# A four-layer Mamba network on one core: six state buffers, the gated output in the gate's tile, second-layer weights before the scans, a first tile without GpSimd products, image edges cleared on VectorE

## The chip, the cores and the metric

The kernel runs on 1 core of one Trainium2 chip. The time of a run is device microseconds of that core; the time of a kernel is the median of several runs. Below, PE is TensorE, DVE is VectorE, ACT is ScalarE, POOL is GpSimd and SP is SyncE, which here only issues DMAs. "Clock" is the share of its full clock that TensorE was granted.

## What is computed

The reference runs four layers, one after the other, on an image batch of 4 x 96 channels x 64 x 64:

- Layers 0 and 2 ("mamba"): each image is a sequence of L = 4096 tokens of 96 channels. Two selective-scan blocks follow each other, then a fusion with pooled channels, a batch norm and a residual.
- Layer 1 ("SSD"): four scans in chunks, over rows and columns, forwards and backwards.
- Layer 3 ("ConvNeXt"): a 7x7 depthwise convolution, a layer norm and an MLP.

The change concerns the selective-scan block, cut here to its core (192 inner channels `d`, 16 states `s`), and the image buffers of layer 3:

```
xz = layernorm(seq) @ in_w;  xs, z = split(xz)
xc = silu(conv4(xs))
dt, Bm, Cm = split(xc @ xproj_w)
delta = softplus(dt @ dt_w + dt_b);  A = -exp(A_log)
dA  = exp(delta[..., None] * A)
dBx = delta[..., None] * Bm[:, :, None, :] * xc[..., None]
h[t] = dA[t] * h[t-1] + dBx[t]                     # for each d and s
y = einsum('blds,bls->bld', h, Cm) + Dp * xc
seq = seq + (y * silu(z)) @ out_w
```

## The kernel before, in words

`program` calls `mamba_fusion`, `ssd`, `mamba_fusion`, `convnext`. Everything is fp32. A framework turns data dependences into semaphores; where tiles of one pool share addresses with tiles of an earlier one, the later ones wait until the earlier are free. Each tile name has a number of buffers (`bufs`); a new tile takes the oldest buffer and waits for that buffer's last readers.

**A mamba layer.** `mamba_fusion` runs 32 steps: 4 images x 2 blocks x 4 pieces of 1024 tokens. A piece is held as two halves of 512 tokens side by side. The 192 x 16 recurrences of a step are 24 groups of 128 (8 channels x 16 states), in three thirds `j`, four quarters `q` and two halves `p`. `Scan.run` writes out by hand the order of one group after another on every engine, and ties it down: in iteration n it emits `load` (group n+5), `spread` (n+1), `decay` (n+2), `after` (n-1), `product` (n+2), `scan` (n), and pieces of the next step's front. For one group:

- `load`, SP: `da`, delta copied to all 16 states by two DMAs from DRAM.
- There are two kinds of group. In 17 of 24, PE spreads `du` = delta*x into the PSUM tile `bs` (`spread`, line 497) and DVE multiplies `bs` by B (line 520); ACT makes exp(A*delta) in `da` (line 110). In the other 7 (`dma` set: p = 1 with even q, and j = 2, q = 1) `du` also comes by two DMAs, POOL multiplies it by B (`product`, line 505), and ACT writes the exponential into `bs`.
- `scan`, DVE, line 525: one TENSOR_TENSOR_SCAN of 1024 elements into a state tile `hs`, of which there are 4 buffers.
- `after`, POOL, line 532: `hc` = `hs` * C; ACT copies the last column into `carry`.
- `sums`, PE, line 546: adds up the states of two groups at a time into the PSUM tile `py`. At the end of a third, `close` (DVE, line 563) multiplies `py` by the gate `z` into a tile `y` (2 buffers), which `project` (PE, line 576) multiplies by `out_w`.

**Before the scans.** `mamba_weights` is a generator that loads and prepares one block's weights: `w_ln`, `w_in`, `w_conv`; then the products on DVE for `w_conv` (line 671), zeroing (675, 681), small loads, `w_dd` (690), the 16 loads of `w_a`, `w_out`, and an exp. For the first block it runs at once; for the second block it is put into `later`, and one of its pieces is emitted in each iteration from group 24 on. `first_front` makes the first step's inputs: `rows` (line 391), the broadcasts `bc` of B and C (`spread`, line 399), the stores of delta and `du` to DRAM (`dd`, `dg`, line 405). `mamba_front` does it for the other steps, under the scans.

**Memory of a mamba layer.** One list in `Laid` gives the order in which tile names lie in SBUF: `h` and the first weights, `dbl`, `delta`, `rs`, `seldu`, `du`, `x`, `ua`, `bc`, `X`, `z`, `hs`, `da`, `y`, `hc`, and the rest.

**Layer 3.** `convnext` holds half-images with a border of 3 in four `band` tiles, each 96 x 2692. Lines 1724 and 1725 set all of each to zero on POOL; `load` then writes the 64 x 64 part (line 1741), for the first half-image on DVE.

Of the kernel before, what the change touches and what calls it, by code (L numbers as in the profile page):

```python
# [18 lines left out]
F32 = mybir.dt.float32  # L19
AF = mybir.ActivationFunctionType  # L20
ALU = mybir.AluOpType
# [4 lines left out]
B, C, HH, WW = 4, 96, 64, 64  # L26
L = HH * WW
P = 128
T = 512
# [16 lines left out]
NQU = QUART // HEIGHT  # L46
GS = 2
# [21 lines left out]
KS = 7  # L69
HALF = KS // 2  # L70
# [100 lines left out]
def mamba_front(tc, k, x_in, pools, wt, parts, c, h, made):  # L171
# [4 lines left out]
    nc = tc.nc  # L176
    work, psum, dram = pools
# [36 lines left out]
    x = made["x"] = work.tile([P, 3, T], F32, name="x", bufs=2)  # L214
    for j in range(3):
        pu = bank("pu")
        for tap in range(4):
            kk = C + 1 if tap == 3 else C
            for i in range(2):
                nc.tensor.matmul(  # L220
                    pu[HALFP * i : HALFP * (i + 1)],
                    lhsT=wt["conv"][:kk, tap, D0[j] : D0[j] + HALFP],
# [5 lines left out]
                    k.act.other(x, x, AF.Silu)  # L228
            yield

    z = made["z"] = work.tile([P, 3, T], F32, name="z", bufs=2)

    def gate(j):
        pz = bank("pz")
# [13 lines left out]
    for j in range(3):  # L248
        for i in range(2):
            half = ds(HALFP * i, HALFP)  # L250
# [71 lines left out]
def first_front(tc, k, x_in, pools, wt, parts, h, made):  # L322

    nc = tc.nc
    work, psum, dram = pools
    nc.vector.memset(h[:C, 0:3], 0.0)

    def bank(tag, bufs):  # L330
        return psum.tile([P, T], F32, tag=tag, name=f"f_{tag}", bufs=bufs)

    xs, into = ([a[:C, ds(of + n * T, T)] for n in range(2)] for a, of in ((x_in, 0), (h, 3)))
    for n, tag in enumerate(("po", "py")):
        pc = bank("mm", 2)[:C]
        nc.tensor.matmul(pc, lhsT=k.center, rhs=xs[n], start=True, stop=True)
        sq = work.tile([P, T], F32, tag="ua", name="sq", bufs=3)[:C]
        nc.scalar.activation(sq, pc, AF.Square)
        pv = bank(tag, 1)[:C]
        nc.tensor.matmul(pv, lhsT=k.mean, rhs=sq, start=True, stop=True)  # L340
        rs = work.tile([P, T], F32, name="rs", bufs=2)[:C]
        rsqrt(k.act, rs, pv, k.eps[:C])
        nc.vector.tensor_tensor(into[n], pc, rs, ALU.mult)
        nc.vector.tensor_scalar(
            into[n], into[n], wt["ln"][:, 0:1], wt["ln"][:, 1:2], ALU.mult, ALU.add
        )

    x, z = (work.tile([P, 3, T], F32, name=m, bufs=2) for m in "xz")
    made["x"], made["z"] = x, z

    def gate(j):
        pz = bank("mm", 2)
        for i in range(2):
            nc.tensor.matmul(
                pz[HALFP * i : HALFP * (i + 1)],
                lhsT=wt["in"][:, DIN + D0[j] : DIN + D0[j] + HALFP],
                rhs=h[:C, ds(3 + i * T, T)], start=True, stop=True,
            )
        k.act.other(z[:, j], pz, AF.Silu, back=False)

    def rows_of(pd, j):
        for i in range(2):
            half = ds(HALFP * i, HALFP)
            nc.tensor.matmul(
                pd[half], lhsT=wt["xproj"][half, j], rhs=x[half, j], start=(j == 0), stop=(j == 2),
            )

    pd = None
    for j in range(3):
        pu = bank("mm", 2)  # L370
        for tap in range(4):
            kk = C + 1 if tap == 3 else C
            for i in range(2):
                nc.tensor.matmul(
                    pu[HALFP * i : HALFP * (i + 1)],
                    lhsT=wt["conv"][:kk, tap, D0[j] : D0[j] + HALFP],
                    rhs=h[:kk, ds(i * T + tap, T)], start=(tap == 0), stop=(tap == 3),
                )
        k.act.other(x[:, j], pu, AF.Silu, back=False)
        if j == 1:  # L380
            gate(0)
    pd = bank("po", 1)
    for j in range(3):
        if j == 2:
            gate(1)
        rows_of(pd, j)
    gate(2)
    dbl = work.tile([P, T], F32, name="dbl")
    nc.vector.tensor_scalar_add(dbl, pd, wt["one"])
    rows = dram.tile([P, T], F32, name="rows")  # L390
    nc.sync.dma_start(rows, dbl)

    bc = made["bc"] = work.tile([P, 2, 2, T], F32, name="bc", bufs=2)
    du = made["du"] = work.tile([P, 3, T], F32, name="du", bufs=2)

    def spread(q):
        for i in range(2):
            r = HALFP * i + (QUART if q else RANK + 1)
            nc.sync.dma_start(
                bc[:, q, i], rows[r : r + NST, None].to_broadcast([NST, HEIGHT, T])  # L400
            )

    def store(name, j, value):
        made[name, j] = dram.tile([P, T], F32, name=f"{name}{j}")
        nc.sync.dma_start(made[name, j], value)

    def sized(j):
        nc.gpsimd.tensor_tensor(du[:, j], deltas[j], x[:, j], ALU.mult)

    deltas = []  # L410
    for j in range(3):
        pt = bank("py", 1) if j == 0 else bank("mm", 2)
        for i in range(2):
            half = ds(HALFP * i, HALFP)
            nc.tensor.matmul(
                pt[half], lhsT=wt["dt"][half, D0[j] : D0[j] + HALFP], rhs=dbl[half], start=True,
                stop=True,
            )
        deltas.append(work.tile([P, T], F32, name="delta", bufs=3))
        k.act.other(deltas[j], pt, AF.Softplus, back=(j == 2))  # L420
        if j == 0:
            store("dd", 0, deltas[0])
            spread(0)
            sized(0)
    for n in range(2):
        unused = work.tile([P, T], F32, tag="ua", name="copy", bufs=3)[:C]
        nc.scalar.activation(unused, xs[n], AF.Copy, accum_out=parts[:, n : n + 1])
    yield
    store("dg", 0, du[:, 0])
    sized(1)  # L430
    yield
    spread(1)
    sized(2)
    yield
    store("dd", 1, deltas[1])
    yield
    store("dg", 1, du[:, 1])
    yield
    store("dd", 2, deltas[2])
    yield  # L440
    store("dg", 2, du[:, 2])
    yield
# [16 lines left out]
class Scan:  # L459
# [55 lines left out]
    def scan(self, g):  # L515
        nc = self.tc.nc
        c, j = g["c"], g["j"]
        da, dbx = g["terms"]
        if not g["dma"]:
            nc.vector.tensor_tensor(dbx, dbx, self.b_or_c(g, 0), ALU.mult)  # L520
        hs = self.state.tile([P, GS, T], F32, name="hs", bufs=4)
        n = g["n"]
        init = 0.0 if c == 0 else self.carry[:, j, n : n + 1]
        out, da, dbx = (x.rearrange("p i t -> p (i t)") for x in (hs, da, dbx))
        nc.vector.tensor_tensor_scan(out, da, dbx, init, ALU.mult, ALU.add)  # L525
        g["hs"] = hs
# [30 lines left out]

    def close(self, g):

        j, made = g["j"], g["made"]  # L560
        if j == 0:
            made["y"] = self.work.tile([P, 3, T], F32, name="y", bufs=2)
        self.tc.nc.vector.tensor_tensor(made["y"][:, j], made["py"], made["z"][:, j], ALU.mult)  # L563

    def project(self, g, i, *parts):


        nc = self.tc.nc
        half = ds(HALFP * i, HALFP)
        for j in parts:  # L570
            if j is None:
                self.po = self.psum.tile([P, T], F32, tag="po", name="po", bufs=1)[:C]
                lhsT, rhs = g["wt"]["of_x"], self.tokens(g, i)
            else:
                lhsT, rhs = g["wt"]["out"][half, j], g["made"]["y"][half, j]
            nc.tensor.matmul(self.po, lhsT=lhsT, rhs=rhs, start=(j is None), stop=(j == 2))  # L576

    def keep(self, g, i):
# [6 lines left out]
    def run(self, steps, wts, front, first, later):  # L585
# [7 lines left out]
        groups = [  # L593
            dict(
                b=b, sub=sub, c=c, wt=wts[sub], made=made[n], j=j, q=q, half=p, n=NQU * p + q,
                last=(q == NQU - 1 and p == 1), dma=(p == 1 and (q % 2 == 0 or (j, q) == (2, 1))),
            )
            for n, (b, sub, c) in enumerate(steps) for j, q, p in units
        ]
# [3 lines left out]
        last = {}  # L603
# [54 lines left out]
def mamba_weights(nc, act, ident, wpool, w, sub, wt):  # L658
# [22 lines left out]
    nc.vector.memset(wt["dt"], 0.0)  # L681
    for b in range(2):
        nc.sync.dma_start(wt["dt"][HALFP * b : HALFP * b + RANK + 1], w["dt"][sub])
    yield
    d = wpool.tile([P, 3, 1], F32, name=f"w_d{sub}")
    for half in HALVES:
        nc.sync.dma_start(d[half, :, 0], w["d"][sub, :HALFP])
# [3 lines left out]
        wt["d"], ident[:, None].to_broadcast([P, 3, P]), d.to_broadcast([P, 3, P]), ALU.mult  # L691
    )

    wt["a"] = wpool.tile([P, 3, HALFP // HEIGHT], F32, name=f"w_a{sub}")
    for s in range(NST):
        nc.sync.dma_start(
# [15 lines left out]
def mamba_fusion(ctx: ExitStack, tc, k, src, dst, w):  # L712
# [1 line left out]
    nc = tc.nc  # L714
    laid = Laid(ctx, tc, "m", (
        "h w_ln0 w_in0 w_conv0 w_xproj0 w_dt0 w_dd0 w_d0 w_a0 w_out0 one7", "dbl", "delta", "rs",
        "seldu", "du", "x", "ua", "bc", "X", "z", "hs", "da", "y", "hc", "*",
    ))
    one = work = state = laid.by(1)

# [96 lines left out]
    gb = one.tile([C, B], F32, name="gb")  # L817
    gpw = one.tile([C, C], F32, name="gpw")

    def other_weights():  # L820

        yield from mamba_weights(nc, k.act, k.ident, one, w, 1, wts[1])
        nc.sync.dma_start(gpw, w["gp_wT"])
        nc.sync.dma_start(fus, w["fus_wT"].rearrange("(q c) o -> c q o", q=2))
        nc.sync.dma_start(vec, w["vecs"])
        yield
# [877 lines left out]
def convnext(ctx: ExitStack, tc, k, src, out, w):  # L1704
# [16 lines left out]

    bands = [one.tile([C, (high + KS - 1) * wide + QUART], F32, name=f"band{i}") for i in range(4)]
    images = [x[:, : (high + KS - 1) * wide].rearrange("c (h w) -> c h w", w=wide) for x in bands]
    for x in bands:
        nc.gpsimd.memset(x, 0.0)
    units = [(b, i) for b in range(B) for i in range(2)]

    def load(n):
# [317 lines left out]
```

## Time and profile before

Three runs gave 8268.09, 8269.03 and 8272.67 us. The profiled execution took 8267.86 us, and the span from its first to its last instruction is 8266.1 us.

| what | where it is from | value |
|---|---|---|
| median of 3 runs | the times | 8269.03 us |
| profiled execution, and its span | the profiled run | 8267.86 us, 8266.1 us |
| mean granted clock | the profiled run | 0.933 |
| first scan of the two mamba layers starts | DVE's timeline | 47.33 us, 5017.03 us |
| their last scan starts | DVE's timeline | 2673.77 us, 7660.65 us |
| POOL busy, whole span | the page's first part | 6790.8 us (82%) |
| ACT busy, whole span | the page's first part | 5208.4 us (63%) |
| one multiplication by C on POOL (line 532), mean | the page's groups | 2.362 us, 1536 times |
| one scan with carry and `bs` (line 525), mean | the page's groups | 2.346 us, 816 times |

How to read the lines shown later: a row of a timeline or of the chain has the start in us, the duration in us, the engine, the line, the operation, and tiles as output<-inputs; in square brackets stands how long the engine was idle just before and what ended that. A row of the windows view gives, for a stretch, the busy time of each engine with the number of its instructions, then the granted clock, the mean busy share of the DMA engines and what they moved. A row of the groups view ends in busy time and mean duration in ns, then the idle time just before these instructions, with what ended it. "issue" means that nothing the profile shows was waited for.

### The profile page before, as it was taken

What the parts mean: (1) busy time and instruction counts of PE and PEld (TensorE: products, weight loads), DVE (VectorE), ACT (ScalarE), POOL (GpSimd) and SP (SyncE); (2) the same over time, 40 slices, a digit from 0 to 9 for tenths busy, and PEclk for the clock granted to TensorE, in tenths of its full rate; (3) what the DMA queues carried; (4) which work ended last, traced back from release to release, by engine and by line L of the source; (5) the groups of instructions that cost most, each with busy time, mean ns of one, the idle gap of its engine ahead of it and who ended that gap; (6) DMA issues with size and microseconds to landing.
All of it is one profiled execution on the core that took longest, in us unless ns stands there. A gap on an engine that the chain in (4) does not pass through costs nothing. (4 is left out here: it accounts for less than half of the span.)

```text
span 8266.1 us, 111696 instructions
## 1 busy us (share of the span) xinstructions
PE 7193.8 (87%) x33944; PEld 3180.7 (38%) x33944; DVE 7532.2 (91%) x8903; ACT 5208.4 (63%) x9494; POOL 6790.8 (82%) x4589
## 2 busy tenths in 40 slices
PE   7888888888887899999999997888888888887688
PEld 2222222222221687888888882222222222221122
DVE  7999999999998799998999997999999999999786
ACT  5566666666664677777777765666666666665255
POOL 6999999999998587887878886999998999998211
PEclk8999999999998899999999998999998999998799
DMA  7989889899987333333333327999888999898453
GB/s 208 238 239 248 235 237 253 233 242 248 236 230 209 101 95 110 111 100 115 94 109 110 95 80 192 238 238 254 232 240 238 239 234 248 236 235 220 118 129 75
DMA packets 819138, 1558.49 MB, mean 189 GB/s; under 512 B 117613, under 2 KB 123529, under 8 KB 815466
## 3 DMA queue, kind: packets, MB, share of 16 engines
q1 hardware_dynamic: 815466, 1546.23, 70.6%
q8 instruction: 272, 4.46, 0.2%
q10 hardware_dynamic: 3072, 5.11, 0.2%
q14 instruction: 328, 2.69, 0.1%
HBM read 1256.10 MB, written 148.50 MB: 170 GB/s over the span
## 5 line engine op out<-in xcount | busy, mean ns | idle before, releaser
L532 POOL TENSOR_TENSOR hc<-hs,bc 128x1024 f32<-128x1024 f32 x1536 | 3604.9, 2362 | 415.6 <-DVE hs L525 349.2
L525 DVE TENSOR_TENSOR_SCAN hs<-da,carry,bs 128x1024 f32<-128x1024 f32 x816 | 1914.7, 2346 | 120.4 <-issue 46.5
L497 PE MATMUL bs<-du,seldu 64*128 64x512 f32 x4352 | 1428.4, 700 | 647.5 <-DVE hs L525 642.6
L520 DVE TENSOR_TENSOR bs<-bs,bc 128x1024 f32<-128x1024 f32 x1088 | 1319.7, 1213 | 118.0 <-PE bs L497 94.6
L110 ACT ACTIVATE da<-da,w_a 128x1024 f32<-128x1024 f32 x1088 | 1231.1, 1140 | 20.7 <-DMA da<-dd 18.3
L505 POOL TENSOR_TENSOR du<-du,bc 128x1024 f32<-128x1024 f32 x448 | 1060.9, 2368 | 24.4 <-DMA du<-dg 14.4
L497 PEld LDWEIGHTS bs<-du,seldu 64*128 64x128 f32 x4352 | 398.0, 200 | 1625.6 <-issue 1155.7
L546 PE MATMUL py<-hc,selsum 128*32 128x512 f32 x6144 | 840.7, 617 | 37.9 <-DVE y L563 24.5
L110 ACT ACTIVATE bs<-da,w_a 128x1024 f32<-128x1024 f32 x448 | 500.2, 1117 | 542.2 <-DVE hs L525 270.3
L220 PE MATMUL pu<-h,w_conv 96*64 96x512 f32 (+1 forms) x2976 | 792.2, 654 | 11.3 <-ACT h L209 11.3
L525 DVE TENSOR_TENSOR_SCAN hs<-bs,carry,du 128x1024 f32<-128x1024 f32 x336 | 781.3, 2325 | 0.0
L525 DVE TENSOR_TENSOR_SCAN hs<-da,bs 128x1024 f32<-128x1024 f32 x272 | 621.9, 2287 | 44.9 <-issue 15.7
L1288 DVE SCALAR_TENSOR_TENSOR bc<-front,taps,bc 128x384 f32<-128x384 f32 (+1 forms) x1152 | 648.4, 563 | 0.5
L1253 PE MATMUL front<-sconv,pk 128*128 128x192 f32 x3072 | 596.4, 331 | 17.3 <-ACT z L1305 11.8
L1413 POOL TENSOR_TENSOR xs<-x,coef 128x576 f32<-128x576 f32 x512 | 590.6, 1153 | 16.3 <-DVE y L1491 14.8
L1482 POOL TENSOR_TENSOR y<-y,xs 128x192 f32<-128x192 f32 x496 | 294.0, 593 | 363.0 <-DVE y L1475 358.5
L1497 ACT ACTIVATE y<-yz 128x192 f32<-128x192 f32 x512 | 183.9, 359 | 554.4 <-DVE yz L1492 477.5
L1382 POOL TENSOR_TENSOR seg<-dr,mask 128x384 f32<-128x384 f32 x512 | 511.4, 999 | 9.6 <-DMA dr<-rows 9.6
L1253 PEld LDWEIGHTS front<-sconv,pk 128*128 128x128 f32 x3072 | 494.5, 192 | 28.3 <-ACT z L1305 18.6
L110 ACT ACTIVATE seg<-seg,ndac 128x128 f32<-128x128 f32 x1536 | 499.3, 388 | 4.2 <-ACT dtrow L1097 1.3
L1838 DVE SCALAR_TENSOR_TENSOR acc<-strips,kern,acc 128x512 f32<-128x512 f32 x504 | 424.4, 844 | 54.9 <-ACT acc L1828 19.8
L115 ACT ACT_TABLE_LOAD x350 | 449.1, 1283 | 8.7 <-ACT dtrow L1097 3.0
(255 smaller groups left out, 12815.1 us busy)
## 6 DMA issues: line engine op xcount, KB each, us to landing
da<-dd SPq DMA_DIRECT2D x3072, 256.0 KB
du<-dg SPq DMA_DIRECT2D x896, 256.0 KB
dr<-rows SPq DMA_DIRECT2D x256, 384.0 KB
bc<-rows SPq DMA_DIRECT2D x256, 256.0 KB
dd<-delta SPq DMA_DIRECT2D x192, 256.0 KB
dg<-du SPq DMA_DIRECT2D x192, 256.0 KB
pk<-xn SPq DMA_DIRECT2D x128, 384.0 KB
pk<-xn SPq DMA_DIRECT2D x128, 256.0 KB
```

Source lines behind the costliest of these rows:

```text
L110: self.last = self.scalar.activation(out, in_, func, **kw)
L220: nc.tensor.matmul(pu[HALFP * i : HALFP * (i + 1)], lhsT=wt["conv"][:kk, tap, D0[j] : D0[j] + HALFP], rhs=h[:kk, ds(i * T + tap, T)], star ...
L497: nc.tensor.matmul(g["bs"][:, i], lhsT=self.sel["du"][rows, g["half"], g["q"]], rhs=g["made"]["du"][rows, g["j"]], start=True, stop=True,)
L505: self.tc.nc.gpsimd.tensor_tensor(g["du"], g["du"], self.b_or_c(g, 0), ALU.mult)
L520: nc.vector.tensor_tensor(dbx, dbx, self.b_or_c(g, 0), ALU.mult)
L525: nc.vector.tensor_tensor_scan(out, da, dbx, init, ALU.mult, ALU.add)
L532: nc.gpsimd.tensor_tensor(g["hc"], hs, self.b_or_c(g, 1), ALU.mult)
L546: nc.tensor.matmul(py[ds(HALFP * i + QUART * x["half"], QUART)], lhsT=self.sel["sum"][:, q], rhs=x["hc"][:, i], start=(q == 0), stop=(q == ...
L1253: nc.tensor.matmul(p, lhsT=held["pk"][:, i, ds(order[m] * Q, Q)], rhs=self.conv[:, i], start=(i == 0), stop=(i == 2),)
L1288: nc.vector.scalar_tensor_tensor(out, shifts[tap], self.taps[:, q, tap : tap + 1], out, ALU.mult, ALU.add)
L1382: self.nc.gpsimd.tensor_tensor(seg, g["pair"]["dr"][:, ds(g["c"] % 2 * NH, NH)], self.mask[:, g["r"]].to_broadcast([P, NH, Q]), ALU.add,)
L1413: self.nc.gpsimd.tensor_tensor(xs, x.to_broadcast([P, 3, NH, HD]), coef.to_broadcast([P, 3, NH, HD]), ALU.mult)
```

## The change

- `hs` has 6 buffers instead of 4.
- The tile `y` is gone. `close` writes `py` * `z` over the third of `z` that it read, `project` reads `z`, and `z` has 3 buffers instead of 2.
- In the list of `Laid`, `z` moves behind `da`, where `y` was.
- In the first step of each mamba layer, groups 1 and 5 (j = 0, q = 0 and 2, p = 1) lose the `dma` mark: no `du` loads and no POOL product; PE spreads and DVE multiplies, as for the other groups.
- In `first_front`, the store of the first `du` follows at once on its product, and the two broadcasts of C (`spread(1)`) are emitted one piece earlier.
- The second block's `mamba_weights` is started ahead of the scans: three pieces, now up to and including `w_dd`, are emitted behind the fetches of `X`. A `yield` moves for this. The rest (`w_a`, `w_out`, exp) stays in `later`.
- In `convnext`, POOL no longer clears the bands. DVE clears the three border rows, the 32 elements behind the image, and the two border columns of 3.

```diff
-    z = made["z"] = work.tile([P, 3, T], F32, name="z", bufs=2)
+    z = made["z"] = work.tile([P, 3, T], F32, name="z", bufs=3)
...
-    x, z = (work.tile([P, 3, T], F32, name=m, bufs=2) for m in "xz")
+    x, z = (work.tile([P, 3, T], F32, name=m, bufs=n) for m, n in (("x", 2), ("z", 3)))
...
             sized(0)
+            store("dg", 0, du[:, 0])
...
     yield
-    store("dg", 0, du[:, 0])
     sized(1)
-    yield
     spread(1)
+    yield
     sized(2)
...
-        hs = self.state.tile([P, GS, T], F32, name="hs", bufs=4)
+        hs = self.state.tile([P, GS, T], F32, name="hs", bufs=6)
...
-        j, made = g["j"], g["made"]
-        if j == 0:
-            made["y"] = self.work.tile([P, 3, T], F32, name="y", bufs=2)
-        self.tc.nc.vector.tensor_tensor(made["y"][:, j], made["py"], made["z"][:, j], ALU.mult)
+        made, z = g["made"], g["made"]["z"][:, g["j"]]
+        self.tc.nc.vector.tensor_tensor(z, made["py"], z, ALU.mult)
...
-                lhsT, rhs = g["wt"]["out"][half, j], g["made"]["y"][half, j]
+                lhsT, rhs = g["wt"]["out"][half, j], g["made"]["z"][half, j]
...
-                last=(q == NQU - 1 and p == 1), dma=(p == 1 and (q % 2 == 0 or (j, q) == (2, 1))),
+                last=(q == NQU - 1 and p == 1), dma=(p == 1 and (q % 2 == 0 or (j, q) == (2, 1)) and (n, j) != (0, 0)),
...
         nc.sync.dma_start(wt["dt"][HALFP * b : HALFP * b + RANK + 1], w["dt"][sub])
-    yield
     d = wpool.tile([P, 3, 1], F32, name=f"w_d{sub}")
...
         wt["d"], ident[:, None].to_broadcast([P, 3, P]), d.to_broadcast([P, 3, P]), ALU.mult
     )
+    yield
...
-        "seldu", "du", "x", "ua", "bc", "X", "z", "hs", "da", "y", "hc", "*",
+        "seldu", "du", "x", "ua", "bc", "X", "hs", "da", "z", "hc", "*",
...
+    second = mamba_weights(nc, k.act, k.ident, one, w, 1, wts[1])
+    for _ in range(3):
+        next(second)
+
     def other_weights():
-        yield from mamba_weights(nc, k.act, k.ident, one, w, 1, wts[1])
+        yield from second
...
-    for x in bands:
-        nc.gpsimd.memset(x, 0.0)
+    for i, x in enumerate(bands):
+        kept = x[:, : (high + KS - 1) * wide]
+        nc.vector.memset(kept[:, -HALF * wide :] if i % 2 else kept[:, : HALF * wide], 0.0)
+        nc.vector.memset(x[:, (high + KS - 1) * wide :], 0.0)
+        for at in (0, HALF + WW):
+            nc.vector.memset(images[i][:, :, at : at + HALF], 0.0)
```

## The prediction, made before the changed kernel ran

> **What bounds the kernel now.** I read the busy time by stage first, then DVE's waits inside a mamba layer, then the costliest groups, then DVE's timeline at single places. The two mamba layers take some 5270 of the 8266.1 us. Their inner stretches by window:
>
> ```profile
> 160.00:2600.00 2440.00, 2101.89 (x8309) 511.31 (x8305) 2320.52 (x1389) 1545.42 (x2295) 2269.61 (x1020) 0.94 0.91 240
> 5210.00:7600.00 2390.00, 2060.45 (x8087) 499.63 (x8084) 2270.95 (x1358) 1500.22 (x2218) 2209.43 (x992) 0.93 0.91 238
> ```
>
> DVE (the third busy time, after PE and PEld) is busy 95%, POOL (the last) 93%. By starts of scans an inner step of 24 groups takes 81.8 us in the first layer, 82.4 in the second. POOL back to back would need 24 x 2.32 + 7 x 2.32 + 3 x 1.23 = 75.6 us (its start-to-start medians), so DVE sets the pace with 6 us to spare. What are DVE's idle 5%?
>
> ```profile
> DVE bs L520 <- PE bs L497: 32.1, 37, 3.3
> DVE hs L525 <- issue: 30.6, 157, 0.5
> DVE bs L520 <- remote: 10.4, 5, 2.2
> ...
> L525 DVE TENSOR_TENSOR_SCAN hs<-da,carry,bs 128x1024 f32<-128x1024 f32 x816 | 1914.7, 2346 | 120.4 <-issue 46.5
> L525 DVE TENSOR_TENSOR_SCAN hs<-bs,carry,du 128x1024 f32<-128x1024 f32 x336 | 781.3, 2325 | 0.0
> ```
>
> The first three lines are DVE's waits in the first stretch, the last two the page's groups. Waits on PE are few and long. The others are many and equal: the scan fed by a DVE product sits idle 120.4 us in all, the scan of the `dma` groups never. No row says that the state buffers are waited for: "POOL hc" releases DVE for 1.9 us in the whole first layer. So by the waits alone, six buffers would be worth nothing.
>
> **Part A: six state buffers.** The worth is in the instruction lists of the two programs. Before, 629 of the 1088 scans fed by a product wait for five semaphores: two DMAs, DVE's own product, ACT, and POOL (the reader of the buffer four groups back). After, 6 do; the others wait for four. The wait for POOL is never late, but it costs an instruction. The timeline shows both kinds side by side:
>
> ```profile
> 5223.27 1.21 DVE L520 TENSOR_TENSOR bs<-bs,bc 128x1024 f32<-128x1024 f32 x1
> 5224.57 2.35 DVE L525 TENSOR_TENSOR_SCAN hs<-da,carry,bs 128x1024 f32<-128x1024 f32 x1
> 5226.83 1.21 DVE L520 TENSOR_TENSOR bs<-bs,bc 128x1024 f32<-128x1024 f32 x1
> 5228.23 2.35 DVE L525 TENSOR_TENSOR_SCAN hs<-da,carry,bs 128x1024 f32<-128x1024 f32 x1 [0.19 <-issue]
> ```
>
> From product to scan it is 1.30 us, then 1.40. In the raw trace all 628 scans with one more separate wait instruction behind the end of the product start 1.397 us (median) after it, the 450 without 1.296. The wait instruction that holds DVE's own semaphore opens only when the product has ended; a fifth semaphore needs one more instruction behind it. So A is at most 623 x 0.101 = 62.9 us.
>
> How much passes? DVE is the pace-setter, but not everywhere. Of its gaps over 0.25 us in the two stretches (91.3 us), 86.6 us lie where the granted clock was halved for at least 30% of the 6 us before; there PE sets the pace, and a saving on DVE becomes a longer wait. Halved time is 307 of 2440 and 348 of 2390 us, 13.6%: at most 8.5 us lost. POOL: its product for group 1 of a step ends 0.48 us (mean) before the scan that reads it, its smallest slack; POOL falls behind from group 15 on, where four scans a step save 0.4 us, so this slack about suffices. I take 58 us, ends 45 and 63.
>
> [...]
>
> **Part B: the second block's weights ahead of the scans.** In the second layer (the first is alike):
>
> ```profile
> 5108.81 2.32 DVE L525 TENSOR_TENSOR_SCAN hs<-bs,carry,du 128x1024 f32<-128x1024 f32 x1
> 5113.38 2.86 DVE L671 TENSOR_TENSOR w_conv<-w_conv,w_in 96x768 f32<-96x768 f32 x1 [2.24 <-DMA w_conv<-in_L_conv_wT]
> 5116.57 1.20 DVE L520 TENSOR_TENSOR bs<-bs,bc 128x1024 f32<-128x1024 f32 x1
> 5123.79 0.67 DVE L563 TENSOR_TENSOR y<-py,z 128x512 f32<-128x512 f32 x1
> 5125.14 2.65 DVE L690 TENSOR_TENSOR w_dd<-ident,w_d 128x384 f32<-128x384 f32 x1 [0.69 <-DMA w_d<-in_L_d]
> 5127.71 1.22 DVE L520 TENSOR_TENSOR bs<-bs,bc 128x1024 f32<-128x1024 f32 x1
> ```
>
> The reader sees DVE stand in its own queue before a DMA, with the scans behind it, and run two products slowly beside POOL (2.86 us against 0.95 for the first block's). Without them line 520 would start at 5111.05 and, 0.58 us behind the start of line 563 as elsewhere, at 5124.37: 5.5 + 3.3 = 8.9 us. In the first layer 141.10 to 146.91 and 154.70 to 155.72: 5.8 + 1.0 = 6.8 us. Sum 15.7 us. Where it goes: DVE 0.95 + 0.56 + 2 x 0.22 = 1.95 us into the idle 12.5 us before line 389 (17.1 in the second layer). On SP 12 DMA issues move from behind `da` loads to between the last `X` fetch (23.1 us) and `rows` (35.4); by their own durations they take some 7.5 us, and SP has nothing else there; nor does POOL's queue. The data land before the `rows` store. If that cover were gone (the product for `w_conv` now stands before line 389), each us late would be a us at the start. Ends 10 (half of the slow products return as waits) and 20 (with two odd waits of 2 us that follow in the second layer).
>
> **Part C: the first tile.** DVE's start:
>
> ```profile
> 53.73 2.29 DVE L525 TENSOR_TENSOR_SCAN hs<-bs,du 128x1024 f32<-128x1024 f32 x1 [2.54 <-POOL du L505]
> 55.94 1.21 DVE L520 TENSOR_TENSOR bs<-bs,bc 128x1024 f32<-128x1024 f32 x1
> 57.23 2.29 DVE L525 TENSOR_TENSOR_SCAN hs<-da,bs 128x1024 f32<-128x1024 f32 x1
> 64.06 1.23 DVE L520 TENSOR_TENSOR bs<-bs,bc 128x1024 f32<-128x1024 f32 x1 [4.54 <-PE bs L497]
> ```
>
> Group 1 waits for two `du` loads and POOL's product. It now follows the two `h` products: line 520 at 51.2, scan at 52.5, line 520 of group 2 at 54.8, scan at 56.1, end 58.4. The stall of 4.54 us stems from `da` of group 2, issued at 49.2 behind the `du` loads and `bc`; ACT and then PE's conv matmuls queue behind it. Its issue moves to about 46, so group 3 begins near 58.9 instead of 64.06. Then PE, at half clock until 65.9, holds DVE about 0.8 us more, and group 5 costs 1.3 us of DVE. Group 6 begins near 70.4, not 73.73: 3.3 us, and much the same in the second layer (stalls 3.33 and 3.54). I take 3.5 each, 7 in all. Lower end -5 (both products cost, no stall goes), upper end 15 (a first step takes 89.2 us; the best inner ones, 78.7, plus two products of 1.3).
>
> **Part D: the bands.** Two clears by POOL run beside the batch-norm statistics:
>
> ```profile
> 7684.95 2.40 DVE L870 TENSOR_SCALAR means<-means,mv 96x32 f32<-96x32 f32 x1
> 7685.10 2.25 DVE L873 TENSOR_REDUCE mv<-sqs 96x1 f32<-96x32 f32 x1
> 7684.98 4.65 POOL L1725 MEMSET band<- 96x2692 f32 x2 [17.21 <-ACT sqs L784]
> ...
> 2699.14 0.24 DVE L870 TENSOR_SCALAR means<-means,mv 96x32 f32<-96x32 f32 x1 [0.72 <-ACT sqs L784]
> ```
>
> The same chain takes 5.1 us here and 2.9 us in the first layer: 2.2 us gained. Of 16 small clears on DVE, one stands before the last scan (0.2 us); seven fill the 4.5 us in which DVE waits for the last `py`; eight stand in the statistics, four of them on the chain: 0.15 us each by the 0.14 to 0.18 of its small rows. Net 2.2 - 0.2 - 0.4 = 1.6 us; ends -1 and 2.
>
> **Moved at no cost.** `close` into `z` has the same shape and the same wait (PE alone). A third `z` buffer only loosens. POOL's `hc` gets a third semaphore 573 times, in the wait instruction it already has; back to back its interval is 2.318 with two semaphores there against 2.311 us, under POOL's slack. Moving `z`, `hs`, `da` in SBUF shifts which SSD tiles wait for them; those loads (`X`, `xn`) start 12 to 30 us before the first use at 2702. If that cover is gone the loss is a few us; kept in the low end of C.
>
> **Sum.** 58 + 15.7 + 7 + 1.6 = 82.3 us. The profiled execution took 8267.9, its span is 1.8 us less; 8267.9 - 82.3 = 8185.6. The median of the runs shown is 1.2 us above that execution, so 8186 us.
>
> **Rivals.**
> 1. *A gives nothing* (10%): the scan is held by something else that ends with the same wait, or POOL's lag takes the place. For: POOL is busy 93%, its least slack 0.48 us. Against: 450 scans with four waits do start earlier, at the same pace of POOL. Time 8267.9 - 24.3 = 8243.6.
> 2. *PE absorbs part* (6%): the waits on PE at half clock grow from 91 by half of A, 30 us, since PE too must do its work in less time. For: PE is busy 86%. Time 8186 + 30 - 5 already counted = 8211.
> 3. *Slower: the granted clock falls* (4%). The same PE work in less time is denser; if the clock answers by more halved stretches, DVE waits more. Price: 86.6 us of waits in 655 us halved, 0.13 us each. It decides once some 620 us more are halved, the mean clock of both layers falling from 0.93 to about 0.87 (1 less half the halved share); at 0.86, 700 us more halved, some 8278 us. Against: in the SSD stage PE is busy 93 to 97% at 0.98 to 1.00.
>
> **How the numbers follow.** The forecast as worked out holds 80%; its own ends are 8267.9 less 63 + 20 + 15 + 2 and less 45 + 10 - 5 - 1: 8168 to 8219. Unlikely all at one end, these hold nine tenths of that case and with rival 2 about 8 in 10; I give 8167 to 8222. A measurement tells 0.2% (17 us) from no change: faster 94% (forecast, rivals 1 and 2, less a little), same 2%, slower 4%.
>
> **What will show it.** Right: the idle time of the scans with carry and `bs` falls from 120.4 to under 15 us; product to scan is 1.30 us nearly always; no line 671 or 690 among the scans; group 6 begins 3 us earlier after the first scan; the batch-norm chain takes 3 us. Wrong: the 0.1 us stays in another wait, the waits on PE grow by tens of us, or the mean clock drops below 0.90.

## The result and the profile after

The changed kernel takes 8356.1 us (median of four runs), the kernel before 8270.9 beside it: a ratio of 1.010, 95% interval 1.0085 to 1.012. It is 85 us slower; 82 us less was forecast. Its profiled execution took 8363.1 us, its span is 8361.2, its mean granted clock 0.914 (before 0.933).

By window, the same two stretches of the mamba layers, with the columns as before (PE, PEld, DVE, ACT, POOL busy, granted clock, DMA):

```profile
160.00:2600.00 2440.00, 2133.10 (x8169) 516.14 (x8166) 2279.88 (x1360) 1516.91 (x2252) 2217.60 (x996) 0.91 0.91 235
5210.00:7600.00 2390.00, 2091.56 (x7962) 505.65 (x7962) 2224.48 (x1327) 1479.53 (x2195) 2166.80 (x973) 0.90 0.90 234
```

DVE and POOL are busy for less, PE for longer with fewer instructions, and the granted clock is 0.03 lower. DVE's waits in the first stretch (us in total, times, longest; "remote" is a wait whose end the profile puts down to nothing it knows):

```profile
DVE bs L520 <- PE bs L497: 72.0, 60, 4.1
DVE bs L520 <- remote: 39.9, 19, 2.2
```

And from the page's costliest groups (busy, mean ns, idle time before and what ended most of it), line 520 of the kernel before first, then two rows of the changed one:

```profile
L520 DVE TENSOR_TENSOR bs<-bs,bc 128x1024 f32<-128x1024 f32 x1088 | 1319.7, 1213 | 118.0 <-PE bs L497 94.6
L525 DVE TENSOR_TENSOR_SCAN hs<-da,carry,bs 128x1024 f32<-128x1024 f32 x816 | 1915.2, 2347 | 72.0 <-issue 0.9
L520 DVE TENSOR_TENSOR bs<-bs,bc 128x1024 f32<-128x1024 f32 x1092 | 1328.6, 1217 | 267.0 <-PE bs L497 172.8
```

The wait of the scans put down to "issue" is gone (46.5 to 0.9 us on the page): part A did what it should at its own place. From product to scan it is now 1.300 us for 1076 scans and 1.39 for 6. But line 520, the product ahead of the scan, which had 118.0 us of idle time before (94.6 by PE), has 267.0. What A gave at the scan was taken back, and more, one instruction earlier, in waits for TensorE.

Where in the step? By starts of scans an inner step takes 83.4 and 84.0 us (81.8 and 82.4 before). DVE's gaps over 0.25 us grew from 1.6 to 4.1 us a step (second layer 1.9 to 4.5), nearly all of it behind the scans of groups 6, 14 and 15. One of them, by window cut on the grid of 3.413 us on which all changes of the granted clock in this trace lie (each within 0.02 us):

```profile
1066.04:1069.45 3.41, 3.41 (x20) 1.07 (x16) 3.32 (x3) 0.86 (x2) 3.41 (x3) 1.00 1.06 277
1069.45:1072.87 3.42, 1.50 (x12) 0.16 (x8) 3.33 (x3) 3.05 (x4) 3.42 (x2) 1.00 1.06 274
1072.87:1076.28 3.41, 2.90 (x6) 0.83 (x8) 3.33 (x3) 0.19 (x1) 3.41 (x3) 0.50 0.98 273
1076.28:1079.69 3.41, 3.41 (x10) 0.98 (x8) 2.74 (x2) 0.57 (x1) 2.19 (x2) 0.50 0.71 186
1079.69:1083.11 3.42, 3.42 (x10) 0.59 (x10) 1.89 (x2) 3.37 (x4) 3.42 (x2) 0.50 0.69 153
1083.11:1086.52 3.41, 3.41 (x17) 0.82 (x18) 2.86 (x2) 2.32 (x5) 2.44 (x2) 1.00 0.18 10
```

PE's timeline in it (start, duration, and the idle time before in brackets):

```profile
1069.89 1.06 PE L546 MATMUL py<-hc,selsum 128*32 128x512 f32 x8
1073.38 2.08 PE L497 MATMUL bs<-du,seldu 64*128 64x512 f32 x4 [2.43 <-DVE hs L525]
1075.39 3.68 PE L220 MATMUL pu<-h,w_conv 96*64 96x512 f32 x8
1079.00 2.08 PE L497 MATMUL bs<-du,seldu 64*128 64x512 f32 x4
```

And DVE's, a little later:

```profile
1081.13 1.23 DVE L520 TENSOR_TENSOR bs<-bs,bc 128x1024 f32<-128x1024 f32 x1 [2.02 <-PE bs L497]
```

This is the whole loss in one picture. At group 4 PE has finished its sums and waits 2.43 us for the scan to free a `bs` buffer. In that stretch of 3.41 us it is busy 1.50 us, 44%. In the next the clock is 0.50, and stays so for three stretches; the spread of line 497 takes 2.08 us instead of 1.13 (the row of the kernel before, below); then DVE waits 2.02 us for the second such spread. Here the clock is halved *after idle time* (the stretch that is 44% busy), not after dense work (the full stretch before it, 3.41 us busy, is followed by one at 1.00). A place in the kernel before, at the same group:

```profile
1134.27:1137.68 3.41, 1.31 (x6) 0.53 (x8) 3.41 (x2) 1.24 (x2) 3.26 (x2) 1.00 1.06 263
1137.68:1141.09 3.41, 3.41 (x10) 0.74 (x8) 3.32 (x3) 0.14 (x1) 3.33 (x2) 0.50 1.05 261
1141.09:1144.51 3.42, 3.42 (x6) 0.75 (x6) 2.30 (x3) 3.37 (x4) 2.32 (x1) 0.50 0.57 161
1144.51:1147.92 3.41, 3.41 (x18) 0.81 (x18) 3.26 (x2) 2.47 (x5) 3.41 (x3) 1.00 0.19 64
```

and PE's row for its idle piece and the spread behind it:

```profile
1136.37 1.13 PE L497 MATMUL bs<-du,seldu 64*128 64x512 f32 x4 [2.61 <-DVE hs L525]
```

Nearly the same idle piece and the same answer, but the first halved stretch is full, and the clock is back sooner. Counted over all stretches of 3.41 us at full clock in the two windows:

```
PE busy share of a stretch   followed by a halved one (before)   (after)
under 45%                     46 of 46                            51 of 51
45 to 65%                     81 of 193                           63 of 140
65% and more                   0 of 984                            0 of 947
first halved stretch busy under 85%: clock back in the next       0 of 15 (before), 0 of 65 (after)
first halved stretch busy 85% and more: back in the next         81 of 111, 30 of 49
```

Other runs show that the bounds are not sharp: in e3_gates, below, 8 of the 984 stretches busy 65% or more, all 8 at 65 to 70%, were followed by a halved one, and in e1_fill one of 14 under 45% (at 42%) was not. The last-but-one row of the table holds in all 14 profiles: of 380 first halved stretches busy under 85% none let the clock back in the next.

Call a run of halved stretches a dip. The number of dips is about the same (128 before, 120 after, in the 30 inner steps of each layer); each lasts longer (most often 3.4 us before, 10.2 after). Halved time in these steps: 680 us before, 1018 after.

### The profile page after: what moved, and what is told of

It is laid out like the page before. It is cut to its first block, busy times and chain, and to the rows that moved or that the text cites. A ratio compares the mean times of both kernels' runs of the same rounds, so it can differ in the third digit from the quotient of the medians.

```text
span 8361.2 us, 111780 instructions
## 1 busy us (share of the span) xinstructions
PE 7334.7 (88%) x33960; PEld 3213.9 (38%) x33960; DVE 7544.8 (90%) x8923; ACT 5210.3 (62%) x9494; POOL 6765.8 (81%) x4581
## 5 line engine op out<-in xcount | busy, mean ns | idle before, releaser
L497 PE MATMUL bs<-du,seldu 64*128 64x512 f32 x4368 | 1501.9, 718 | 609.2 <-DVE hs L525 604.4
L520 DVE TENSOR_TENSOR bs<-bs,bc 128x1024 f32<-128x1024 f32 x1092 | 1328.6, 1217 | 267.0 <-PE bs L497 172.8
L497 PEld LDWEIGHTS bs<-du,seldu 64*128 64x128 f32 x4368 | 421.6, 207 | 1611.9 <-issue 1231.7
L546 PE MATMUL py<-hc,selsum 128*32 128x512 f32 x6144 | 868.0, 636 | 27.0 <-DVE z L561 14.5
L574 PE MATMUL po<-z,w_out 64*96 64x512 f32 x768 | 473.1, 716 | 0.0
```

Source lines behind the costliest of these rows:

```text
L497: nc.tensor.matmul(g["bs"][:, i], lhsT=self.sel["du"][rows, g["half"], g["q"]], rhs=g["made"]["du"][rows, g["j"]], start=True, stop=True,)
L546: nc.tensor.matmul(py[ds(HALFP * i + QUART * x["half"], QUART)], lhsT=self.sel["sum"][:, q], rhs=x["hc"][:, i], start=(q == 0), stop=(q == ...
```

## The experiments

Three theories were set against each other: G, called the gate (stretches of 3.413 us in which TensorE idled are followed by halved ones, as counted above, and A moves the idle pieces against these stretches; that some 40% of idle time is enough is the author's estimate: after the change 113 of the 183 stretches busy under 60% were followed by a halved one); Q, the buffers themselves hold POOL or TensorE; S, the shifted start alone does it. In every kernel with "fill", the added matmuls add zeros. The table has medians, the ratio to the kernel before run beside it (its medians 8262 to 8271 us), and from the profiled execution the mean inner step of both layers and the halved time in the inner steps.

```
kernel                              us       ratio (95%)             step us      halved us
before                             8270.9    1                       81.8, 82.4    680
after                              8356.1    1.010 (1.0085 1.012)    83.4, 84.0   1018
e1_hs4          four buffers       8244.7    0.9975 (0.9965 0.9986)  81.6, 81.7    617
e1_onlyA        part A alone       8345.9    1.010 (1.0086 1.0117)   83.0, 83.8    945
e1_fill         after + fill       8129.8    0.984 (0.9826 0.9859)   79.5, 79.6     58
e1_before_fill  before + fill      8213.1    0.994 (0.9928 0.9957)   80.6, 80.7    116
e2_hs4_fill     four + fill        8193.5    0.991 (0.9898 0.9927)   80.5, 80.4    119
e2_busy         fill, busy places  8700.8    1.053 (1.0509 1.055)    89.4, 89.8    884
e2_pause        tiny clear         8223.2    0.996 (0.9942 0.997)    80.7, 82.0    641
e4_slow         larger clear       8296.4    1.003 (1.0013 1.0049)   82.4, 83.2    802
e3_half         half the fill      8112.6    0.9815 (0.9801 0.983)   79.5, 79.5     76
e2_best         fill + last steps  8112.1    0.981 (0.9798 0.9827)   79.5, 79.8     61
e3_gates        gates moved        8158.4    0.987 (0.9854 0.9887)   80.5, 80.4    601
e3_gates_fill   moved + some fill  8164.3    0.988 (0.9865 0.9899)   80.4, 80.6    338
```

(The expectations count halved time in the two windows of the prediction, some 655 us before and 940 after; the table counts the dips that start in the 30 inner steps of each layer.)

**Which part does it: e1_hs4 and e1_onlyA.**

```
-        hs = self.state.tile([P, GS, T], F32, name="hs", bufs=6)
+        hs = self.state.tile([P, GS, T], F32, name="hs", bufs=4)
```

> The changed kernel with four state buffers again; the rest of the change stays. Three theories. G (gate): TensorE's clock is halved after a stretch of 3.41 us in which TensorE idled for more than some 40%; six buffers speed DVE up, so TensorE's idle pieces fall otherwise against these stretches and each halved time lasts longer. Then it goes back: 8268 - 24 = about 8244 us, halved time in the two stretches of the layers about 650 us (938 with the whole change). Q (queue): with six buffers POOL runs further behind and TensorE is held by that; the same 8244 us. S (start): the weights and the first tile shift everything by some us against the clock's windows, the buffers have no part in it; then it stays slow, about 8356 + 62 = 8418 us, and some 940 us halved.

e1_onlyA is the kernel before with the diff's lines on `hs`, `z`, `close` and the order in memory, and nothing else.

> The kernel before with part A alone: six state buffers, gated output in z's place, the three z buffers and the new order in memory. G and Q: the loss is there without the other parts: 8356 + 24 = about 8380 us, some 940 us halved. S: faster than before by A's 58, about 8210 us, some 650 us halved.

8244.7 and 8345.9 us: with four buffers the loss is gone, with six it is there without the other parts. S falls. e1_onlyA is 34 us faster than G and Q let expect, though: the other three parts are worth 20 us by e1_hs4 (0.9975, its interval leaving 9 us either way), but with six buffers nothing of them shows (1.0101 without them, 1.0103 with them).

**Filling the idle time: e1_fill and e1_before_fill.**

```
+FILL = {0: 2, 4: 2, 12: 2, 20: 2}
...
+            if g := at(3):
+                for _ in range(FILL.get(n % each, 0)):
+                    self.tc.nc.tensor.matmul(
+                        g["made"]["py"], lhsT=self.sel["nil"], rhs=g["hc"][:, 0],
+                        start=False, stop=False,
+                    )
```

> The changed kernel with more work for TensorE: behind the sums at groups 0, 4, 12 and 20 of each step two more matmuls 128x128x512 that add zeros to py, some 1.06 us at the full clock, 4.2 us a step, 270 us in all. G: they lie in TensorE's idle time and keep its stretches above the threshold: mean clock of the layers 0.97 or more, line 520's waits for PE under 60 us (172.8 now), and the kernel gets faster by the work added: under 8230 us. Q and every theory by which TensorE has too much to do: slower, 8370 us or more.

> The kernel before with the same matmuls added. G: the halved time of its layers (650 us) mostly goes and with it most of the 86.6 us of DVE's waits that lie there: about 8190 us. Without the gate: not faster, 8268 us or more.

More work made both kernels faster: the changed one from a ratio of 1.010 to 0.984, the one before to 0.994. e1_before_fill, at 8213.1 us, gained less than the 78 us expected. The windows of e1_fill (the second ends at 7400 us here):

```profile
160.00:2600.00 2440.00, 2237.90 (x8903) 576.79 (x8899) 2367.27 (x1420) 1562.36 (x2317) 2317.49 (x1042) 0.99 0.92 244
5210.00:7400.00 2190.00, 2032.79 (x8182) 524.16 (x8178) 2146.73 (x1290) 1434.04 (x2122) 2102.58 (x944) 1.00 0.94 247
```

And its page, the products and the added matmuls:

```profile
L521 DVE TENSOR_TENSOR bs<-bs,bc 128x1024 f32<-128x1024 f32 x1092 | 1321.1, 1210 | 50.5 <-PE bs L498 44.9
L650 PE MATMUL py<-hc,nil 128*128 128x512 f32 x1024 | 520.3, 631 | 0.0
```

The clock is at 0.99 to 1.00, DVE busier than in either kernel (97% of the first stretch), and the products' wait for PE fell from 172.8 to 44.9 us although PE got 520 us of matmuls more (by the page's busy time). That is twice the 270 us of the expectation: each of the 512 added matmuls is two instructions of the profile and takes about 1.0 us of PE, not 0.53. Q and "too much for TensorE" fall.

**A control, and the price of A: e2_busy and e2_hs4_fill.** The first has the table `{5: 2, 6: 2, 14: 2, 15: 2}`; the second is e1_hs4 with the fill of e1_fill.

> A control for the added matmuls: the changed kernel with the same eight a step, but at groups 5, 6, 14 and 15, where TensorE has no idle time. G: the idle stretches at 0, 4, 12 and 20 stay and with them the halved time; the work comes on top where DVE waits for TensorE already: slower than the changed kernel, 8400 to 8650 us. If any added work helps (a mere change of phase): below 8300 us.

> Four state buffers, the rest of the change, and the added matmuls at 0, 4, 12 and 20: what A is worth once the clock is held. If the prediction's price was right and only the clock ate it: 8130 + 58 = 8188 us. If A has no worth of its own: 8130 us.

e2_busy took 8700.8 us, beyond the end of what was expected: the same eight matmuls a step in busy places leave 884 us halved and make DVE wait. Its waits in the first stretch (160 to 2600 us; 72.0 after the change):

```profile
DVE bs L521 <- PE bs L498: 237.8, 115, 5.0
```

So it is the place of the added work that counts. e2_hs4_fill took 8193.5 us. With the clock held, then, A is worth (0.9912 - 0.9842) x 8264 = 58 us, B, C and D together (0.9943 - 0.9912) x 8264 = 26 us, and the whole change 83 us (8213.1 - 8129.8). The intervals of the ratios leave 17 to 18 us either way on each of the three, and the clock is not held quite equally (119, 116 and 58 us halved).

**Is it DVE's pace? e2_pause and e4_slow.**

```
         if not g["dma"]:
+            nc.vector.memset(self.sel["nil"], 0.0)
             nc.vector.tensor_tensor(dbx, dbx, self.b_or_c(g, 0), ALU.mult)
```

> The changed kernel, six buffers kept, with one more tiny instruction on DVE ahead of each of the 1092 products (a clear of one column), so that DVE is slower again by about the 0.1 us that A took away. G (the gate; DVE's pace decides how TensorE's idle pieces fall): the halved time of the layers falls from 938 us towards 650 us and the kernel with more work is faster than the changed one: 8240 to 8320 us. Q (six buffers hold TensorE or POOL back, whatever the pace): the halved time stays near 940 us and the added work comes on top: 8356 + 60 to 110 = 8415 us or more.

> The clear of one column cost DVE only some 0.02 us a product, so it was no test of the pace. Here it clears 40 columns, by the 0.15 us of a 114-column clear some 0.06 us a product and 1.0 us a step, as much as A took away (623 x 0.1 us over 64 steps); six buffers stay. Pace theory (what A gave DVE per step decides the rhythm): back to the rhythm of four buffers, some 81.6 us a step, 600 to 650 us halved, 8230 to 8260 us. Accident theory (any small shift of the rhythm can break or make the long halved times): the time is anywhere between 8180 and 8360 us and the halved time need not be near that of four buffers. Q (the buffers themselves): 8415 us or more.

`nil` is 128x1 in the first, 128x40 in the second. e2_pause's premise failed: the clear overlaps the product, and a group costs some 0.03 us more, not 0.1 (3.59 us from scan to scan where it was 3.56, medians). All the same it is some 120 us faster than the changed kernel (0.9956 against 1.0103), with the six buffers in place: that rules out Q a second time. e4_slow takes some 0.05 us a group from DVE (3.61), 0.8 us a step where A gave 1.0. It did not return to the 8245 us of four buffers, but came to 8296.4 us and 802 us halved: the accident theory's case, not the pace theory's. Which rhythm sets in cannot be read off DVE's pace. The time does follow the halved time: with six buffers, all four parts and no change to PE's work, 641 us halved go with 8223.2 us, 802 with 8296.4 and 1018 with 8356.1.

**How much is needed, and without added work: e3_half, e3_gates, e3_gates_fill, e2_best.** e3_half has `{0: 1, 4: 1, 12: 1, 20: 1}`. e3_gates adds nothing and moves two gate products in the front:

```
+EARLY = {(0, 3): 1, (2, 1): 2}
...
+            if (j, tap) in EARLY:
+                gate(EARLY[j, tap])
...
     sized(0)
-    gate(1)
     yield
     store(0)
-    gate(2)
     yield
```

> Half the dose: the changed kernel with one zero-adding matmul (0.53 us) instead of two at groups 0, 4, 12 and 20. G, with a threshold between 45% and 62% busy in a stretch of 3.41 us: stretches of 38 to 45% come to 54 to 60%, so a part of the dips stays: halved time 200 to 500 us, time between 8130 and 8250, about 8180 us. If any addition, however small, broke the pattern: 8130 us.

> The changed kernel with no work added: of the next step's front the two gate products (pz of j = 1 and 2, 1.08 us each at the full clock) move from groups 14 and 15, where DVE waits for TensorE, to the idle pieces at groups 0 and 4. G: the dips at 0 and 4 go, those at 12 and 20 stay; halved time of the layers from 938 to about 400 us, time about 8190 us (between 8356 and the 8130 of all four places filled). If only added work or a slower pace helped: 8330 us or more.

> The same with zero-adding matmuls only at groups 8 (one), 12 and 20 (two each), and in the last step of a layer as before. G: as few dips as with all places filled, 2.1 us less work for TensorE per step: 8090 to 8115 us (8112 with all places filled).

> The changed kernel with the added matmuls, one more at group 8 (the largest idle piece left, 1.7 us a step) and two at each group of the last step of a layer at which py is open, where no front gives TensorE work. G: most of the dips left in the layers go, the two last steps lose some 6 us each: 8110 to 8130 us, against 8130 with the first table. Otherwise: the same or slower.

The half dose does as much as the whole (76 us halved, 8112.6 us): more than was expected. Its size was reckoned too low: one added matmul takes about 1.0 us of PE (520.3 us for 512 in e1_fill), not 0.53, so by estimate a stretch rises by some 0.3 of its 3.41 us. In it stretches of 55 to 65% busy were followed by no halved one (0 of 107), while after the change 49 of 94 such stretches were; the share in a stretch is thus not the whole condition. e3_gates was faster than expected (8158.4, 8190 expected) with more halved time than expected (601 us, some 400 expected), so here G's price does not fit: the moved work left a new idle piece at group 16 (1.2 us a step). But DVE's gaps at groups 6 and 15 are gone, and at 14 0.9 and 0.6 us a step are left of 1.4 and 1.5: where the clock is still low, PE has less to do there. How much of its gain is the clock's and how much that relief was not measured apart. e3_gates_fill missed (8164.3, 8115 at most expected): nothing was added at 16, where PE's idle piece is 2.0 us a step, and 338 us stay halved. e2_best hit (8112.1). e2_best and e3_half beat the kernel before by 1.9%.

## Why the prediction was wrong

**Part A, at its place: right.** 1.397 went to 1.300 us, and with the clock held the whole part is worth 58 us, the value taken (that it is met to the us is luck, given 18 us either way). One sign for it was set wrongly: 0.09 us lie between the recorded end of a product and a scan behind it even with four waits (1.296 less 1.21 us), some 70 us for 816 scans, so that their idle time could not fall under 15 us; the 72.0 measured is about the floor.

**"How much passes?": this step failed.** It counted the halved time as given, 13.6% of the stretches, and let at most 8.5 us of A be lost there. But the halved time answers to the kernel: it grew by 338 us (680 to 1018), and DVE's gaps over 0.25 us from about 105 to 258 us over the inner steps (1.58 + 1.92 against 4.09 + 4.50 us, 30 steps each). That alone turns a gain of 82 us into a loss: 82 - 153 = -71, against the 85 measured; the 14 us between are not explained.

**Rival 3 named the right quantity with the wrong cause and price.** It let the clock fall because PE's work becomes denser. The profile shows the opposite: no stretch busy 65% or more was followed by a halved one (0 of 984 before). That stood in the trace of before, and the figures cited against the rival (SSD, PE 93 to 97% busy at 0.98 to 1.00) said it too. In the traces of before and after the granted clock changes only on a grid of 3.413 us (its 354 and 328 pieces at one clock all begin within 0.02 us of it), and idle time of 1.92 us in a stretch of 3.42 was enough for a halved one behind it (1069.45 to 1072.87 above: 1.50 us busy). The price of 0.13 us per halved us held for short dips (before: 105 / 680 = 0.15); in long ones it is 258 / 1018 = 0.25. DVE's gaps per dip show it: before, 0.2 us on average at a dip of one stretch, 1.0 at two, 2.6 at three; after, 2.8 at three. So 338 us more sufficed, where 620 were asked for.

**Rival 2** (PE absorbs part of A) had PE as a fixed limit. With the clock held PE takes the added matmuls and still leaves DVE 97% busy: at its full clock it was not short of time.

**Parts B, C and D: right in sum as far as measured, not shown one by one** (24.3 predicted; 20 and 26 us measured, with 9 and 17 us either way, and nothing beside e1_onlyA). From the first scan to the start of the third step e1_hs4 takes 7.1 us less than before in the first layer and 15.6 in the second. But e1_onlyA, which has none of the three parts, takes 12.2 us less there too, and e1_before_fill 8.9, so most of the 15.6 cannot be put down to them. In the first layer 2.4 us go off, since the first scan starts later (49.7 for 47.3). Here the cover named for B was thinner than thought. The changed kernel's timeline:

```profile
45.44 1.23 DVE L520 TENSOR_TENSOR bs<-bs,bc 128x1024 f32<-128x1024 f32 x1 [4.95 <-DMA bc<-rows]
49.01 2.29 DVE L525 TENSOR_TENSOR_SCAN hs<-da,bs 128x1024 f32<-128x1024 f32 x1 [2.34 <-ACT da L110]
```

The product was free to start at 43.99 before; now it waits for `bc`, issued only 0.2 us later than before but landed at least 1.4 us later. The scan itself waits for ACT on `da`, whose loads are issued 0.5 us later (41.66 for 41.16) and whose exponential begins 1.7 us later (47.83 for 46.15): that is the whole delay (49.01 for 47.33). That the second block's weights are still in the queues is a possible cause; it wasn't tried. e1_onlyA, without B and C, starts its first scan at 47.1; the kernels that have them start it anywhere from 47.2 to 49.7. In C, group 6 begins 2.5 and 3.1 us earlier after the first scan (3.3 and 3.5 taken); in the first layer the later first scan takes most of that away (1.7 us in the changed kernel). In D the batch-norm chain takes 3.3 us, not 5.2; at the end of the kernel 0.6 us of it is left.

**What stays open.** What decides that a dip lasts one stretch or three is only half known: no first halved stretch under 85% busy let the clock back (0 of 380), and in the changed kernel the idle piece runs over the edge of the stretch (1072.87 in the picture above), so that the first halved one is not full. Its steps then repeat in fours, 82.0 + 84.6 + 82.7 + 85.3 = 334.6 us, which is 98 stretches of 3.413. That the steps fall into step with the clock is argued from this sum; e2_pause and e4_slow show only that small shifts change the outcome by 60 to 120 us. How six buffers bring about the longer dips is thus not shown, only that they do (e1_hs4, e1_onlyA) and that the loss goes when PE's idle pieces are filled (e1_fill, e3_half). The exact condition between 45 and 65% is not found.

## What to carry to other kernels

Ask of a halved clock what PE did in the stretch before it (3.41 us in these traces). After the change all 51 stretches busy under 45% were followed by a halved one, and none of the 947 busy 65% and more: here the clock was a consequence of the schedule, and a saving on another engine made the time longer (e1_onlyA, a ratio of 1.010). Count idle pieces per stretch before pricing a saving on the engine that sets the pace; where pieces like the 2.43 and 2.61 us shown above recur, put other work there (or matmuls that add zeros) first, and measure the saving then: with the clock held the terms of this change added up to 83 us of the 82 forecast, with 18 us either way. Without that, kernels with the same six buffers that differ by a clear of a few columns lay between 8223 and 8356 us.

## What was not expected of the hardware

Adding 512 matmuls made a kernel whose TensorE is busy 88% faster by 2.6% (8356.1 to 8129.8 us; the percentages are from the ratios to the kernel before); half of them by 2.9%. A clear of one column ahead of each of 1092 products, some 0.03 us each, made it faster by 1.5%. The runs of one kernel agree all the same (8351.5 to 8363.1 us for the changed one).
